# A gated recurrence in which every matrix product is cut into four 32-column groups of 128 columns, r and z take seven block products for eight, and a list scheduler orders the engines

## The chip, the core and the metric

The kernel runs on one core of one Trainium2 chip. A core has five engines with an instruction queue each: TensorE (PE, matrix products), VectorE (DVE), ScalarE (ACT), GpSimd (POOL) and SyncE (SP, which here only issues transfers). Queues run side by side and are worked off in order; semaphores join them. The metric is device time in microseconds, and lower is better. All data are 32-bit floats.

A matmul takes a stationary operand (here up to 128 rows by 32 columns, loaded by a LDWEIGHTS) and streams a moving operand of N columns past it. The kernel always uses 32 stationary columns, because half of the batch has 32 rows. Four such products can stand side by side in TensorE, each in its own *column group* of 32 columns, and each writes its own quarter of the 128 partitions of PSUM. A 32-bit matmul stands in the trace as two records, each with a weight load.

## The reference

Batch 64, 128 time steps, input and hidden width 512. With `comb = [x_t, h]`:

```python
def step(h, inp):
    x_t, prop = inp
    comb = jnp.concatenate([x_t, h], axis=-1)
    z = jax.nn.sigmoid(comb @ Wz + bz)
    r = jax.nn.sigmoid(comb @ Wr + br)
    comb2 = jnp.concatenate([x_t, r * h], axis=-1)
    h_cand = jnp.tanh(comb2 @ Wh + bh)
    h_new = (1.0 - z) * h + z * h_cand
    h_next = jnp.where(prop, jnp.tanh(h_new @ Wp + bp), h_new)
    return (h_next, h_new)
```

`prop` holds in every fourth step but the last. The result is `x` plus all `h_new`. The part with `x_t` of the three gates doesn't depend on `h` and can be worked out ahead; the part with `h` is a chain of 128 steps.

## The kernel before, in words

**Layout.** The batch is two halves of 32 rows (`S = 2`, `V = 32`), the hidden width four quarters of 128 columns (`NQ = 4`, `J = 128`). A state tile is 128 partitions (32 rows times four quarters) by two halves by 128 columns. K, the 512 rows of a weight, is four blocks of 128.

**The recurrence.** `half(h)` (L777) is a generator that runs the whole chain for one half of the batch: gate r, then r times h and its 32x32 transposition (L794, L244), gate z, gate of the candidate, the new state (L831, L840) and its transposition, and in every fourth step the propagation with `wp`. `gate` (L224) calls `products` (L213) for each of four blocks of K; `products` issues two matmuls of 256 columns (L215) into the two column groups 2h and 2h+1. One half of the batch therefore fills two of the four groups, and the other half has the other two. `seed` (L377) copies the prepared part of x into the PSUM bank ahead of the gate (L380). `crossed` (L239) applies sigmoid or tanh in two calls of 64 partitions, which bring the partitions back to the state's layout (L241).

**The part with x.** Steps 0 to 3 and the last ones use plain products (`plain`, L435: 48 matmuls a step). All other steps are done in groups of four (`Q4`) by a block scheme used twice, one inside the other, with seven products for eight: 49 block products for a group. `batch` (L453) runs two outer products at a time, each with seven inner ones, as matmuls of 192 columns into the banks `scratch`; ACT and DVE add the seven results up (L484, L501, L502, L507, L510, L511), and POOL makes the outer sums, with the biases, into `cp` (L542, L547). The sums of x that go into the products are POOL's too (`four`, L307).

**Order.** The two generators are interleaved by hand: at each yield the half with fewer columns issued so far goes on, with a lag of 700 columns (L868). Between the gates each half puts batch units into its own two groups (`fill`, L398), as many as the tables `PLACES`, `HEAD` and `TAIL` (L590) say for the step of the period of eight. Work of POOL and DVE is placed by step in `join` and `behind_step`. Loads of x are blocks of four steps, stores of the result likewise, all issued by SP except for some at the start that POOL and ACT issue.

Of the kernel before, what the change touches and what calls it, by code (L numbers as in the profile page):

```python
# [11 lines left out]
U16 = mybir.dt.uint16  # L12
AF = mybir.ActivationFunctionType
ALU = mybir.AluOpType
PSUM = bass.MemoryType.PSUM


@with_exitstack
def kernel(
# [14 lines left out]
    nc = tc.nc  # L34
# [8 lines left out]
    K = D // P  # L43
    Q4 = 4
    CHUNK = 4
    FIRST = 2
    LAST = T // Q4 - 1
# [3 lines left out]

    const = ctx.enter_context(tc.tile_pool(name="const", bufs=1))
    xrp = ctx.enter_context(tc.tile_pool(name="xr", bufs=2))  # L60
    one = ctx.enter_context(tc.tile_pool(name="one", bufs=1))
    xtp = ctx.enter_context(tc.tile_pool(name="xt", bufs=2))
    mbp = ctx.enter_context(tc.tile_pool(name="mb", bufs=3))
    two = ctx.enter_context(tc.tile_pool(name="two", bufs=2))
# [3 lines left out]
    zeros = one.tile([P, 4 * J], BF16, tag="cq", name="zeros")  # L68
    nc.vector.memset(zeros, 0.0)
    ones = const.tile([1, V], F32, name="ones")  # L70
    nc.gpsimd.memset(ones, 1.0)

    wx = const.tile([P, K, 3, H], F32, name="wx")
    wh = [const.tile([P, K, H], F32, name=f"wh_{i}") for i in range(3)]
    wp = const.tile([P, K, H], F32, name="wp")

    tw = {n: const.tile([P, S, NQ, 3, J // 2], F32, name=f"tw_{n}") for n in (2, 3, 4, 5)}
    tf = {n: const.tile([P, NQ, 3, J // 4], F32, name=f"tf_{n}") for n in (1, 2, 3)}
    tt = const.tile([P, 7, 3, NQ, 3, J // 4], F32, name="tt")
    gates_in = (Wr, Wz, Wh)  # L80

    bias_row = tt.rearrange("p a b c d e -> p (a b c d e)")[0:1, : 3 * H].rearrange(
        "p (i n) -> p i n", i=3
    )
# [4 lines left out]
    def load_x(tile_, t0, n):  # L89
        for h in range(S):  # L90
            for q in range(NQ):
                nc.sync.dma_start(
                    out=tile_[part(q), 0:n, h, :], in_=x[ts(h, V), t0 : t0 + n, ts(q, J)]
                )

    def load_step(t, engs):
        for q in range(NQ):
            engs[q % len(engs)].dma_start(
                out=xr[0][part(q), t], in_=x[:, t, ts(q, J)].rearrange("(h b) j -> b h j", h=S)
            )  # L100

    def load_wx(wt, w, k0=0, k1=K):
        nc.sync.dma_start(  # L103
            out=wt[:, k0:k1, :], in_=w.rearrange("(p k) n -> p k n", k=K)[:, k0:k1]
        )

    def load_wh(wt, w, engs=(nc.sync,)):
        for q in range(NQ):
            engs[q % len(engs)].dma_start(  # L109
                out=wt[part(q)], in_=w[ts(q, P), :].rearrange("(k e) n -> e k n", e=V)  # L110
            )

    xr = {}

    def new_xr(g):
        xr[g] = xrp.tile([P, Q4, S, J], F32, tag="xr", name=f"xr_{g}")

    h_init = two.tile([P, S, J], F32, tag="h", name="h_init")
    bias_x = const.tile([P, C, S, 3, J // 2], F32, name="bias_x")
    bias_p = const.tile([P, S, J], F32, name="bias_p")  # L120
    new_xr(0)
    load_step(0, (nc.sync, nc.scalar))
    for k in range(0, K, 2):
        load_wx(wx[:, :, R, :], gates_in[R][:D], k, k + 2)
    for i in (Z, H_):
        load_wx(wx[:, :, i, :], gates_in[i][:D])

    load_step(1, (nc.gpsimd,))
    for i, b in enumerate((br, bh, bz)):
        nc.gpsimd.dma_start(out=bias_row[:, i, :], in_=b.rearrange("(o n) -> o n", o=1))  # L130
    for t in (2, 3):
        load_step(t, (nc.gpsimd,))
    for h in range(S):
        nc.gpsimd.dma_start(
            out=h_init[:, h, :],
            in_=h0[ts(h, V), :].rearrange("b (q j) -> q b j", q=NQ),
        )

    nc.gpsimd.tensor_copy(wh[R][0:1, 0, 0:1], wx[0:1, K - 1, H_, 0:1])
    for i in range(3):  # L140
        load_wh(wh[i], gates_in[i][D:], (nc.sync, nc.gpsimd))

    dummy = const.tile([1, 1], F32, name="dummy")
    nc.scalar.activation(dummy, ones[:, 0:1], AF.Sigmoid)

    xs = {}

    def load_xs(g):
        if g * Q4 < T:
            xs[g] = one.tile([P, Q4, S, J], F32, tag=f"xs{g % 2}", name=f"xs_{g}")  # L150
            load_x(xs[g], g * Q4, Q4)

    new_xr(1)
    load_x(xr[1], Q4, Q4)
    load_xs(2)
    load_wh(wp, Wp)
    for q in range(NQ):
        nc.sync.dma_start(
            out=bias_p[part(q)],
            in_=bp.rearrange("(o d c j) -> c o d j", o=1, d=2, c=2)[q % 2].broadcast_to(  # L160
                [V, S, J]
            ),
        )


    P_ = 3
    rec = [ps_c.tile([P, 2, 2, J], F32, name=f"rec_{n}") for n in ("0", "1", "z")]
    z = rec[2][:, 1]

    def gate_ps(i, h):  # L170
        return rec[2][:, 0] if i == Z else rec[h][:, 0 if i == R else 1]

    scratch = [ps_c.tile([P, 4 * J], F32, name=f"scratch_{n}") for n in "qraxy"]
    q_ps, r_ps, a_ps, *x_two = (
        s[:, : 3 * J].rearrange("p (m h v) -> p m h v", m=2, h=S) for s in scratch
    )
    q_bank, r_bank, a_bank, *x_banks = range(5)
    r_ = scratch[r_bank][:, 3 * J :]

    def quarters(v):  # L180
        return v.rearrange("p n (d c j) -> p c n d j", d=2, c=2)

    def spread(bank, rows, which):
        bank = bank.rearrange("p (i d j) -> p i d j", i=2, d=2)
        for h in range(S):
            for c in range(2):
                nc.tensor.matmul(
                    bank[part(2 * h + c), 0 : len(which)],
                    lhsT=ones,
                    rhs=quarters(bias_row[:, rows])[:, c],  # L190
                    start=True,
                    stop=True,
                )
        for j, i in enumerate(which):
            nc.scalar.copy(
                bias_x[:, :, :, i, :].rearrange("p n d u -> p d n u"),
                bank[:, j].rearrange("p d (n u) -> p d n u", n=C),
            )

    bias0 = bias_x[:, 0]  # L200
    bias_d = const.tile([P, S, 3, J // 2], F32, name="bias_d")

    def idle(n):
        for i in range(n):
            nc.tensor.matmul(
                rec[i // NQ % 3].rearrange("p a d n -> p (a d n)")[part(i % NQ)],
                lhsT=zeros[:, :V],
                rhs=zeros,
                start=True,
                stop=True,  # L210
            )

    def products(ps, h, left, rhs, start=False):  # L213
        for c in range(2):
            nc.tensor.matmul(  # L215
                ps[part(2 * h + c)],
                lhsT=left,
                rhs=rhs(c),
                start=start,
                stop=True,  # L220
                skip_group_check=True,
            )

    def gate(i, h, lT, w):  # L224
        for k in range(K):
            products(gate_ps(i, h), h, lT[:, h, ts(k, V)], lambda c: quarters(w)[:, c, k])
            yield S * J

    def product(ps, h, lT, w, k, start=False):
        c0, s0 = divmod(k, C)  # L230
        products(
            ps.rearrange("p (d j) -> p d j", d=2),
            h,
            lT[:, c0, s0 * B + h * V : s0 * B + (h + 1) * V],
            lambda c: quarters(w)[:, c, k],
            start,
        )

    def crossed(dst, h, i, func):  # L239
        for d in range(2):  # L240
            nc.scalar.activation(dst[ts(d, 2 * V)], gate_ps(i, h)[ts(h, 2 * V), d, :], func)  # L241

    def turn(dst, src):
        nc.vector.transpose(out=dst, in_=src)  # L244

    def new_T(tag, name):
        return two.tile([P, S, P], F32, tag=tag, name=name)

    xT = {}

    def join_x(g, i):
        if g * Q4 >= T:
            return
        if g not in xT:
            xT[g] = xtp.tile([P, Q4, C, P], F32, tag="xT", name=f"xT_{g}")
        src = xr[g] if g < FIRST else xs[g]
        nc.vector.transpose(
            out=xT[g][:, i].rearrange("p c (a h b) -> p h (c a) b", a=S, h=S),
            in_=src[:, i].rearrange("p h (e k) -> p h k e", k=K),
        )  # L260

    def outer(kb, nb, ka):
        return wx[:, kb * S + ka, :, :].rearrange("p g (q n u) -> p n q g u", q=NQ, n=C)[:, nb]

    OPERAND = {
        1: lambda ka: outer(0, 0, ka),
        2: lambda ka: outer(1, 0, ka),
        3: lambda ka: outer(1, 1, ka),
        4: lambda ka: tw[4][:, ka],
        5: lambda ka: tw[5][:, ka],  # L270
# [649 lines left out]
```

## Time and profile before

| | |
|---|---|
| runs | 1275.79, 1276.58, 1276.74 us; median 1276.58 |
| span of the profiled execution | 1273.0 us, 60669 instructions |
| mean granted TensorE clock | 0.997 |
| busy share | PE 99%, weight loads 90%, DVE 63%, ACT 66%, POOL 71% |
| DMA | 60.82 MB, mean 48 GB/s |

The profile is one execution. The page gives only its span (first to last instruction) and no time of its own beside it; 1273.0 us stand against the runs above. In a group's row stand the source line, engine, operation, output and input tiles with their shapes and the count, then busy time and the mean duration of one in ns, then idle time of the engine before them and what ended it. A row of a stretch has its bounds, its length, the busy time and count of PE, of weight loads, DVE, ACT and POOL, then the granted clock, the DMA share and GB/s. A row of a timeline has start, duration, engine, line and operation, and in brackets the idle time before it. Rows of waits have the total, how many, and the longest. A matmul's record starts when it starts, but its end is modelled: in a stream of matmuls the distance of two starts is what one costs.

### The profile page before, as it was taken

How to read it: one execution, taken by the hardware profiler on the slowest of the kernel's cores; microseconds unless marked ns; L12 is line 12 of the kernel's file. 1: busy time of each engine (PE TensorE's matmuls, PEld its weight loads, DVE VectorE, ACT ScalarE, POOL GpSimd, SP SyncE). 2: the span in 40 equal slices, each digit the busy share in tenths (PEclk: the TensorE clock that was granted, in tenths of full speed). 3: DMA queues.
4: the chain of work that ended last, by engine and by line, in shares of the span. 5: the costliest groups of instructions: out<-in, count | busy, mean ns of one | idle time of the engine just before them, and what ended most of it. 6: DMA issues, size and time to landing. Idle time of an engine off the chain costs nothing.

```text
span 1273.0 us, 60669 instructions
## 1 busy us (share of the span) xinstructions
PE 1255.9 (99%) x25954; PEld 1150.3 (90%) x25954; DVE 800.4 (63%) x2153; ACT 835.5 (66%) x2685; POOL 906.0 (71%) x1053
## 2 busy tenths in 40 slices
PE   7899999999999999999999999999999999999998
PEld 4699999999999999999999999999999999999885
DVE  2765666666666666666666665666666666666544
ACT  1356666766666666676666667666666666666665
POOL 8788767777677786777687677776777777677530
PEclk9999999999999999999999999999999999999999
DMA  8302212102121111211111121111111112111010
GB/s 233 76 19 53 52 41 60 40 24 49 53 53 36 36 47 42 53 36 44 49 32 53 46 59 37 29 43 53 53 37 37 48 39 52 37 52 35 4 50 21
DMA packets 112212, 60.82 MB, mean 48 GB/s; under 512 B 12776, under 2 KB 108520, under 8 KB 111944
## 3 DMA queue, kind: packets, MB, share of 16 engines
q1 hardware_dynamic: 110532, 54.71, 16.5%
q8 instruction: 205, 3.36, 1.1%
q0 software_dynamic: 1120, 2.11, 0.7%
q14 instruction: 63, 0.52, 0.1%
q10 hardware_dynamic: 292, 0.13, 0.0%
HBM read 40.11 MB, written 16.78 MB: 45 GB/s over the span
## 4 chain that ended last, share of the span: by engine, by line
PE 95%; DMA 2%; DVE 1%; issue 1%; SPq 0%; ACT 0%; POOL 0%; POOLq 0%; DVEq 0%
PE rec L215 43%; PE rec_z L215 16%; PE scratch_r L215 14%; PE scratch_q L215 10%; PE scratch_a L215 5%; PE scratch_x L215 4%; PE scratch_y L215 4%; DMA wh<-in_L_cond_Wh_dram 1%; DMA wx<-in_L_cond_Wh_dram 1%; DVE tw L292 0%; DVE tw L293 0%; DVE tw L291 0%; SPq L109 0%; ACT rec_z L241 0%; SPq L103 0%
## 5 line engine op out<-in xcount | busy, mean ns | idle before, releaser
L215 PE MATMUL rec<-wh,rhT 128*32 128x256 f32 x4096 | 373.2, 379 | 0.0
L215 PE MATMUL rec<-wh,hT 128*32 128x256 f32 x3072 | 281.1, 381 | 4.9 <-DVE hT L244 4.7
L215 PE MATMUL rec_z<-wh,hT 128*32 128x256 f32 x3072 | 280.0, 379 | 0.1
L215 PEld LDWEIGHTS rec<-wh,rhT 128*32 128x32 f32 x4096 | 241.2, 110 | 23.4 <-ACT scratch_r L241 1.3
L241 ACT ACTIVATE scratch_r<-rec 64x128 f32<-64x128 f32 x512 | 128.0, 250 | 136.0 <-PE rec L215 68.1
L380 ACT COPY rec<-cp 64x256 f32<-64x256 f32 x512 | 189.8, 371 | 23.6 <-DVE cp L418 4.2
L215 PEld LDWEIGHTS rec<-wh,hT 128*32 128x32 f32 x3072 | 175.0, 110 | 27.3 <-ACT rec L380 6.4
L215 PEld LDWEIGHTS rec_z<-wh,hT 128*32 128x32 f32 x3072 | 184.8, 110 | 7.3 <-issue 0.6
L241 ACT ACTIVATE rec_z<-rec_z 64x128 f32<-64x128 f32 x512 | 128.0, 250 | 93.7 <-PE rec_z L215 81.6
L241 ACT ACTIVATE c<-rec 64x128 f32<-64x128 f32 x512 | 139.3, 272 | 60.1 <-PE rec L215 48.9
L215 PE MATMUL scratch_r<-tw,s 128*32 128x192 f32 x1392 | 166.0, 326 | 0.0
L752 POOL TENSOR_TENSOR xr<-xr,h 128x256 f32<-128x256 f32 x127 | 93.2, 734 | 89.6 <-DVE h L840 89.6
L542 POOL TENSOR_TENSOR mb<-mb,mb 128x768 f32<-128x768 f32 x58 | 106.3, 1833 | 66.4 <-DVE mb L511 66.4
L542 POOL TENSOR_TENSOR cp<-mb,mb 128x768 f32<-128x768 f32 x76 | 139.2, 1832 | 18.7 <-ACT scratch_r L241 9.4
L542 POOL TENSOR_TENSOR cp<-mb 128x768 f32<-128x768 f32 x46 | 84.3, 1834 | 59.7 <-ACT rec_z L380 58.3
L810 DVE SCALAR_TENSOR_TENSOR keep<-rec_z,h 128x256 f32<-128x256 f32 x96 | 40.8, 425 | 123.6 <-ACT rec_z L241 122.5
L484 ACT COPY cq<-scratch_q 128x384 f32<-128x384 f32 x212 | 102.3, 482 | 19.4 <-PE scratch_q L215 17.8
L501 DVE TENSOR_TENSOR cx<-scratch_r,cx 128x384 f32<-128x384 f32 x106 | 58.5, 552 | 74.3 <-PE scratch_r L215 40.3
L215 PE MATMUL scratch_q<-tt,s 128*32 128x192 f32 x928 | 101.9, 326 | 0.0
L215 PEld LDWEIGHTS scratch_r<-tw,s 128*32 128x32 f32 x1392 | 90.7, 110 | 7.7
L507 DVE TENSOR_TENSOR mb<-scratch_q,cx 128x384 f32<-128x384 f32 x106 | 58.8, 555 | 58.8 <-ACT cq L484 58.8
L794 DVE TENSOR_TENSOR rh<-scratch_r,h 128x128 f32<-128x128 f32 x192 | 56.0, 292 | 62.3 <-ACT scratch_r L241 62.3
(168 smaller groups left out, 3718.0 us busy)
## 6 DMA issues: line engine op xcount, KB each, us to landing
out_dram<-xr SPq DMA_DIRECT2D x249, 64.0 KB, 1.8
xr<-in_x_dram SPq DMA_DIRECT2D x248, 64.0 KB, 2.1
xs<-in_x_dram SPq DMA_DIRECT2D x240, 64.0 KB, 2.1
wx<-in_L_cond_Wr_dram SPq DMA_DIRECT2D x2, 512.0 KB, 5.5
wx<-in_L_cond_Wz_dram SPq DMA_DIRECT2D x1, 1024.0 KB
wx<-in_L_cond_Wh_dram SPq DMA_DIRECT2D x1, 1024.0 KB
wp<-in_L_cond_Wp_dram SPq DMA_DIRECT2D x4, 256.0 KB, 6.2
wh<-in_L_cond_Wr_dram SPq DMA_DIRECT2D x2, 256.0 KB, 4.3
```

What stands on the lines that cost most here:

```text
L215: nc.tensor.matmul(ps[part(2 * h + c)], lhsT=left, rhs=rhs(c), start=start, stop=True, skip_group_check=True,)
L241: nc.scalar.activation(dst[ts(d, 2 * V)], gate_ps(i, h)[ts(h, 2 * V), d, :], func)
L380: nc.scalar.copy(gate_ps(i, h)[rows].rearrange("p d (c n) -> p d c n", c=C), G[t][rows, :, :, i, :].rearrange("p c d n -> p d c n"),)
L484: nc.scalar.copy(c[:, :nm], ps[:, :nm])
L501: nc.vector.tensor_add(T2[what][:, :nm], r_ps[:, :nm], T2[what][:, :nm])
L507: nc.vector.tensor_add(blocks(1, 1), runs(q_ps[:, :nm]), runs(T2[what][:, :nm]))
L542: nc.gpsimd.tensor_add(dst, a, b)
L752: nc.gpsimd.tensor_add(xr[g][:, j], xr[g][:, j], h_new)
L794: nc.vector.tensor_mul(rh[:, h, :], r_, h_old[:, h, :])
L810: nc.vector.scalar_tensor_tensor(out=keep, in0=z, scalar=1.0, in1=h_old, op0=ALU.subtract, op1=ALU.mult)
```

## The change

Nearly the whole body is rewritten. What it does:

- *Four groups for each product.* A product of 32 rows with one block of K is four matmuls of 128 columns, one for each column group (`product_k`, `plain`), and a batch product is four matmuls of 96 columns for each half. Gate results thus stand in the state's layout: one activation call reads all 128 partitions.
- *Seven for eight.* From step 4 on, r and z of both halves are one block product: left, the two halves of the batch (`e`, `l`) by two halves of K; right, the weights of r and z by two halves of K. `gates_seven` uses seven block products with four differences of the state on POOL (`sa`), sums of weights made once (`s1`, `wt`, and `wh` of z overwritten by a difference), and six sums on DVE. Steps 0 to 3 keep `gates_plain`.
- *Batches.* Sums inside a batch are now partly made by seeding a PSUM bank with a copy of another (ACT) and accumulating on top; three of seven batches have their biases seeded into the banks, which takes most of POOL's bias sums away. Only steps 0 to 3 have plain products of x; the last group is a batch too.
- *Order.* Every operation is an `Op` of a `Plan` with engine, estimated cost, the data that it reads and writes, PSUM banks, and a due time in steps. `close` finds the dependences, `order` goes through the operations engine by engine: it takes the one that is due first among those that can start soonest, favours the chain (`main`) by 0.3 steps, keeps batch units back that are due more than one step after the next chain operation of PE, and lets an engine wait a little for a chain operation rather than begin a long one. Then all are emitted in that order, and each engine's order is fixed.
- *Transfers.* x is loaded for one step and half at a time, once for the products (`xj`) and once for the result (`xo`), each in a ring of four; results are stored by step and half.

```diff
-    def products(ps, h, left, rhs, start=False):
-        for c in range(2):
-            nc.tensor.matmul(
-                ps[part(2 * h + c)],
-                lhsT=left,
-                rhs=rhs(c),
...
-    def crossed(dst, h, i, func):
-        for d in range(2):
-            nc.scalar.activation(dst[ts(d, 2 * V)], gate_ps(i, h)[ts(h, 2 * V), d, :], func)
...
-    LAG = 700
-    halves = [half(0), half(1)]
...
+class Plan:
...
+    def order(self, patience, ahead, favour):
...
+        def urgency(op):
+            return op.due - (favour if op.main else 0.0) - op.rank
...
+                    if n < len(line_):
+                        limit = line_[n].due + ahead
+                        line = [op for op in line if op.main or op.due <= limit]
...
+                starts = [(begin(op), op) for op in line]
+                early = min(s for s, _ in starts)
+                picks = [(urgency(op), op.index, s, op) for s, op in starts if s <= early + 0.03]
...
+    COST = {
+        "dve": {64: 0.23, 128: 0.325, 256: 0.45, 384: 0.585},
+        "act": {128: 0.30, 256: 0.40, 384: 0.51},
+        "pool": {64: 0.36, 96: 0.40, 128: 0.48, 192: 0.60, 256: 0.76, 384: 1.1, 768: 1.86},
+    }
...
+    def product_k(ps, lT, w, ks, start, reads=(), writes=(), banks=""):
+        def emit():
+            for n, (kl, kw) in enumerate(ks):
+                for q in range(NQ):
+                    dst, right = ps[part(q)], w[:, kw, ts(q, J)] if w is not None else s1(kw)[:, q]
+                    if w is None:
+                        dst = dst.rearrange("p (d u) -> p d u", d=2)
+                    mm(dst, lT[:, ts(kl, V)], right, start and n == 0)
+
+        plan.due += 0.01
+        add("pe", 0.219 * len(ks), emit, reads, writes, banks, main=True)
...
+                    def unit(left=left, right=right, m=m, first=first):
+                        for h in range(S):
+                            for q in range(NQ):
+                                mm(ps[bank][part(q), m, h].rearrange("p (g u) -> p g u", g=3),
+                                   left[:, ts(h, V)], right[:, q], first and h == 0)
...
+        seeded("q", bias_q)
+        product("q", 1, bias is None)
+        copy(ps["a"], ps["q"], [key["q"]], [key["a"]], "q +a")
+        seeded("r", bias_r)
+        product("r", 5, bias is None)
+        copy(c5, ps["r"], [key["r"]], [("c5", n)], "r")
+        product("q", 6, False)
+        product("a", 2, False)
+        copy(block(0, 0), runs(ps["a"]), [key["a"]], blocks(0, 0), "a")
+        copy(ps["x"], ps["q"], [key["q"]], [key["x"]], "q +x")
+        copy(q2, ps["q"], [key["q"]], [("q2", n)], "q")
...
+    def gates_seven(t):
...
+        seed(cn(R_), xpart(t, R, 1), gx[R], [("R", 0)], "r")
+        product_k(B_, e, wh[R], first, True, reads=he + wk(R, 0, 1), writes=[("B", 0), ("E", 0)], banks="+b")
+        plus(cn(A_), cn(B_), xpart(t, R, 0), [("B", 0)] + gx[R], [("A", 0)], "b +e")
+        product_k(A_, e, wh[R], second, False, reads=he + [("A", 0)] + wk(R, 2, 3), writes=[("A", 0)], banks="+e")
+        reset(t, 0)
+        s(0, l[:, :B], e[:, :B], he + hl)
+        s(1, l[:, B:], sa[:, 0], hl + [("sa", t, 0)])
+        product_k(R_, l, S4, [(2, 0), (3, 1)], False, reads=hl + [("R", 0), ("T", 0, 4)], writes=[("R", 0)], banks="+r")
+        plan.due += 0.01
+        el("act", 128, lambda: nc.scalar.copy(c2_(t), R_), [("R", 0)], [("c2", t)], "r", main=True)
+        p(E_, "E", 0, None, [("T", 0, 1)])
+        p(B_, "B", 1, S2, [("T", 0, 2)])
+        plus(c2_(t), E_, c2_(t), [("E", 0), ("c2", t)], [("c2", t)], "b")
+        plus(R_, B_, c2_(t), [("B", 0), ("c2", t)], [("R", 0)], "b +r")
+        s(2, l[:, B:], l[:, :B], hl)
+        s(3, e[:, B:], sa[:, 1], he + [("sa", t, 1)])
+        reset(t, 1)
+        p(B_, "B", 2, wh[Z][:, 0:KH], [("T", 0, 3)])
+        plus(cn(c3_(t)), cn(E_), xpart(t, Z, 1), [("E", 0)] + gx[Z], [("c3", t)], "b")
+        plus(zz[:, 1], B_, c3_(t), [("B", 0), ("c3", t)], [("z", 0, 1)], "b +z")
+        p(B_, "B", 3, wh[Z][:, KH:K], wk(Z, 2, 3))
+        plus(cn(zz[:, 0]), cn(B_), xpart(t, Z, 0), [("B", 0)] + gx[Z], [("z", 0, 0)], "b +z")
...
+    plan.close()
+    plan.order({"pool": (0.1, 3.0), "dve": (0.15, 0.7), "act": (0.15, 0.5), "pe": (0.05, 0.08)}, 1.0, 0.3)
+    stats(plan)
+    for op in plan.done:
+        op.emit()
```

The products of `gates_seven` are called by their banks below: product 1 (`B_`, state `e`), the second r product (`A_`), the S4 product (`R_`, state `l`), E and B2 (`E_`, `B_` with `sa` 0 and 1), and the two last ones into `B_` for z. A *unit* is the eight matmuls of one batch product for both halves.

More of the change, by code (lines that the diff above doesn't have):

```diff
@@ L18, with stats @@
+def stats(plan):
+    import os, pickle
+    if os.environ.get("PLAN_OUT"):
+        pickle.dump([(o.engine, o.cost, o.start, o.end, o.main, o.index, sorted(o.after), o.name) for o in plan.done],
+                    open(os.environ["PLAN_OUT"], "wb"))
 @with_exitstack
@@ L113 @@
[L113 to L126, printed above, removed]
@@ L143 @@
[L143 to L161, printed above, removed]
-            ),
-        )
@@ L243, in turn, with mm @@
[L243 to L259, printed above, removed]
+    def mm(dst, lhsT, rhs, start):
+        nc.tensor.matmul(dst, lhsT=lhsT, rhs=rhs, start=start, stop=True, skip_group_check=True)
```

1434 lines of the change are left out of this document (817 added, 617 removed), and 4 rows, old and new, of the table RINGS.

## The prediction

> **What bounds the kernel now.** I read the engine totals first, then the chain that ended last, then the stretches of the span, and last the single matmuls.
>
> ```profile
> PE 1255.9 (99%) x25954; PEld 1150.3 (90%) x25954; DVE 800.4 (63%) x2153; ACT 835.5 (66%) x2685; POOL 906.0 (71%) x1053
> PE 95%; DMA 2%; DVE 1%; issue 1%; SPq 0%; ACT 0%; POOL 0%; POOLq 0%; DVEq 0%
> ```
>
> TensorE is busy for 99% of the span and is 95% of the chain. A busy PE need not be one at its peak, so the stretches (time, PE busy, weight loads, DVE, ACT, POOL, clock) come next.
>
> ```profile
> 0.00:6.50 6.50, 4.63 (x42) 1.60 (x42) 0.92 (x2) 1.49 (x2) 5.14 (x14) 1.00 0.63 176
> 6.50:46.00 39.50, 30.15 (x492) 17.85 (x496) 18.54 (x30) 7.36 (x24) 31.62 (x34) 0.96 0.86 213
> 130.00:1130.00 1000.00, 1000.00 (x20980) 935.24 (x20976) 647.37 (x1753) 683.13 (x2192) 734.87 (x858) 1.00 0.17 44
> 1220.00:1273.00 53.00, 47.23 (x842) 35.26 (x834) 24.73 (x78) 30.25 (x105) 10.30 (x10) 0.99 0.11 27
> ```
>
> From 130 to 1130 us PE never idles; a record takes 47.7 ns of the span. Lost time lies at the head and in the last steps. What does one record cost when all four groups of 32 columns work? Two places tell: plain products at the head (256 columns) and a stretch where both halves run batches (192 columns; ten such rows stand from 52.01 to 53.47, each with one record for each of two groups).
>
> ```profile
> 14.53 1.91 PE L215 MATMUL scratch_a<-wx,xT 128*32 128x256 f32 x32
> 16.25 1.26 PE L215 MATMUL scratch_r<-wx,xT 128*32 128x256 f32 x20
> 52.01 0.36 PE L215 MATMUL scratch_x<-tt,s12r 128*32 128x192 f32 x2
> 53.47 0.36 PE L215 MATMUL scratch_r<-tf,s12r 128*32 128x192 f32 x2
> ```
>
> 256 columns: 1.72 us for 32 records, 53.8 ns each, 215 ns in one group. 192 columns: 1.46 us for nine periods, 162 ns in one group, 40.6 ns for each record. So a record costs 0.207 ns a column plus 0.8 ns, shared by four groups. By the loops the kernel has 13,856 records of 256 columns (two for each of 6,928 matmuls) and 12,040 of 192: 745 + 488 = 1,234 us of matmul in a span of 1,273. The bound is the number of columns streamed, and 39 us are lost around it.
>
> **The change, part by part: matmul time.** Seven products of two weight blocks replace r's and z's eight from step 4 on: 56 matmuls of 128 columns where 64 would stand. With candidate (32 a step), propagation (31 times 32), four plain steps (384) and four steps of x (384) that is 12,672 matmuls, 25,344 records. The batches are 1,526 units of eight matmuls of 96 columns, 24,416 records. No record of 128 or 96 columns is in this trace. By the line above they cost 27.3 and 20.7 ns: 692 + 505 = 1,197 us, **37 us less**. (The eighth product is worth 124 x 16 x 27.3 ns = 54 us; twice as many records give back some 19 us of the constant.) In the steady part that is 74.4 us for eight steps, against 76.6 us of records now.
>
> From below, the same columns cannot be cheaper than 0.207 ns each, which would save the 40 us of constants more. From above stand 215/4 = 54 ns a record, if a record had no price below 256 columns, which is 2,690 us; nearer floors are a rival below. I take the line, because the next rows show neither issue nor weight load as slow as 20 ns.
>
> ```profile
> 45.44 0.31 DVE L244 STREAM_TRANSPOSE hT<-h 128x128 f32<-128x128 f32 x1
> 45.67 0.27 DVE L831 TENSOR_TENSOR rec_z<-c,rec_z 128x128 f32<-128x128 f32 x1
> 45.90 0.41 PE L215 MATMUL rec<-wh,hT 128*32 128x256 f32 x2 [4.75 <-DVE hT L244]
> 45.91 0.41 PE L215 MATMUL scratch_a<-wx,xT 128*32 128x256 f32 x2
> 45.93 0.11 PEld L215 LDWEIGHTS rec<-wh,hT 128*32 128x32 f32 x1
> 45.94 0.12 PEld L215 LDWEIGHTS scratch_a<-wx,xT 128*32 128x32 f32 x2
> 45.98 0.29 DVE L840 TENSOR_TENSOR h<-rec_z,keep 128x128 f32<-128x128 f32 x1
> 600.95 0.39 PE L215 MATMUL rec_z<-wh,hT 128*32 128x256 f32 x2
> 601.39 0.25 ACT L241 ACTIVATE rec_z<-rec_z 64x128 f32<-64x128 f32 x1 [0.31 <-PE rec_z L215]
> ```
>
> After a wait, four matmuls start within 0.02 us, and second weights begin 0.03 us later, each group for itself. The same rows price a handoff. The transposition ends at 45.75, the matmul starts at 45.90: **0.15 us into PE**. Last matmul's start to its reader is **0.44 us** at 256 columns; at 128 the record is 106 ns shorter, so 0.33. A 128-column product over two blocks of K is 4 x 109 = 0.44 us of PE and 0.66 us from its start to its reader; over four blocks 0.87 and 1.09. DVE instructions follow each other after some 0.03 us.
>
> **The other engines.** Rows for the durations:
>
> ```profile
> L244 DVE STREAM_TRANSPOSE hT<-h 128x128 f32<-128x128 f32 x254 | 79.2, 312 | 8.8
> L507 DVE TENSOR_TENSOR mb<-scratch_q,cx 128x384 f32<-128x384 f32 x106 | 58.8, 555 | 58.8 <-ACT cq L484 58.8
> L794 DVE TENSOR_TENSOR rh<-scratch_r,h 128x128 f32<-128x128 f32 x192 | 56.0, 292 | 62.3 <-ACT scratch_r L241 62.3
> L810 DVE SCALAR_TENSOR_TENSOR keep<-rec_z,h 128x256 f32<-128x256 f32 x96 | 40.8, 425 | 123.6 <-ACT rec_z L241 122.5 <-PE rec L215 1.0
> L241 ACT ACTIVATE scratch_r<-rec 64x128 f32<-64x128 f32 x512 | 128.0, 250 | 136.0 <-PE rec L215 68.1 <-DVE mb L510 52.8 <-DVE cx L501 1.5
> L380 ACT COPY rec_z<-cp 128x256 f32<-128x256 f32 x128 | 48.2, 377 | 55.7 <-DVE h L840 52.5 <-DVE cp L418 2.2 <-POOL cp L542 1.0
> L484 ACT COPY cq<-scratch_q 128x384 f32<-128x384 f32 x212 | 102.3, 482 | 19.4 <-PE scratch_q L215 17.8
> L542 POOL TENSOR_TENSOR cp<-mb,mb 128x768 f32<-128x768 f32 x76 | 139.2, 1832 | 18.7 <-ACT scratch_r L241 9.4 <-DVE mb L511 5.8
> L547 POOL TENSOR_TENSOR mb<-mb,bias_x 128x768 f32<-128x768 f32 x34 | 62.3, 1831 | 28.3 <-DVE mb L511 28.3
> L311 POOL TENSOR_TENSOR s4r<-xT 128x64 f32<-128x64 f32 x29 | 9.5, 327 | 0.0
> ```
>
> DVE gains six 128-column sums a step (nearest row 292 ns): 124 x 6 x 0.292 = 217 us, and loses three of five 384-column sums for each of 106 batches (318 x 0.555 = 176 us): 841 us busy, and with some 2,570 gaps of 0.03 us 918, or 7.2 us a step. ACT gains three copies a batch and 90 copies that seed biases into banks (408 x 0.48 = 197 us), and loses half of its activations, because a call now reads all 128 partitions at once (seven fewer a step, 128 x 7 x 0.25 = 224 us): about even. POOL loses some 60 bias sums (110 us) and gains four 64-column subtractions a step for the seven products (496 x 0.327 = 162 us). SP issues 788 transfers for 765, loads in rings of four tiles well ahead of use. None of these passes PE's 9.35 us a step (1,197/128), so I cost them at nothing as work; PE hides them. If that cover goes, they cost through the recurrence, which is next.
>
> **The recurrence.** The kernel orders each engine beforehand, so I follow one step. In the instruction order a middle step is: product 1, a batch unit (0.33 us), the S4 product, the second r product, E, B2, a unit, candidate of the first half, a product, a unit, candidate of the second half, the last product, then some eight units. From the last product (start) to the next step's first: reader 0.66, z sum 0.29, sigmoid 0.36 (between 250 and 377 ns), keep 0.43, product 0.29, difference 0.29, transposition 0.31, gaps 0.2, into PE 0.15, together 3.0 us. PE has the product itself (0.44) and eight units (2.65): 3.1, covered. The S4 product waits for the second half's new state, which DVE delivers three instructions (0.98 us) later; product and one unit cover 0.77, so 0.2 is open where one unit stands there, nothing where two do. E's operand takes POOL 0.33 us from the same state, and E starts 0.87 us after S4: covered, as long as POOL isn't in a 1.83 us sum. Candidate one: second r product 0.66, sigmoid 0.28, product 0.32, transposition 0.31, into PE 0.15, sum 1.7 after its start; PE has 3 x 0.44 + 0.33 = 1.65. So 0.2 to 0.3 us are open; I take 0.25 for each of 116 steps, **29 us**. Ends: none (the middle stretch now), and 1.2 us a step, if all eight handoffs paid 0.15.
>
> The last batch is due by step 123, so the last four steps stand bare. Their loop: into PE 0.15, product 0.66, sum 0.29, into PE 0.15; B2 starts 0.87 later, 2.1. Reader 2.8, DVE first ends r's first half, then two sums, 3.4; sigmoid, product, transposition, into PE: 4.5. Candidate 0.87, last product's reader 0.66: 6.0; then sum, sigmoid, keep, product, difference, transposition with gaps: 8.2 us. PE's work in it is 88 x 2 x 27.3 ns = 4.8 us, so 3.4 us x 4 = **14 us** idle.
>
> Head: the first matmul waits for the same transfers (6.5 us). Then come all four plain x steps, 21 us of work, during which the recurrent weights land; now PE waits for these instead.
>
> ```profile
> PE rec L215 <- DMA wh<-in_L_cond_Wr_dram: 2.8, 1, 2.8
> PE scratch_q L215 <- DMA wx<-in_L_cond_Wr_dram: 1.4, 2, 0.8
> ```
>
> I keep 4 us for loads and 6 us for steps 0 to 3, which stand almost without batch units; ends 2 and 20 (now: 39.5 us with 492 x 53.8 ns = 26.5 us of work). After the last matmul 6 us, as now.
>
> **The sum.** 6.5 + 1,197 + 4 + 6 + 29 + 14 + 6 = 1,263 us of span, against 1,273.0. The page gives the profiled execution no time beside its span; the span stands 3.6 us below the median of the runs (1,276.58), so I predict **1,267 us**. A measurement of this kernel can tell about 0.2%, 2.6 us, from no change.
>
> **Rivals.**
>
> Slower: *DVE brings the turned state late.* One queue, loaded for 7.2 of 9.35 us a step, now carries six more sums a step in a fixed order; one 0.55 us evacuation in front of a transposition, of which PE covers 0.1, lifts the open time from 0.25 to 0.70 us a step: +52 us, 1,319. It decides from 0.35 us a step on, where the 10 us gained are gone. For it: DVE's waits in the rows above are for ACT, so it works just in time. Against: DVE has idle time in every step.
>
> *All handoffs are covered*: no open time in the middle, 1,263 - 29 = 1,234, 1,238 us. For it: the middle stretch now idles nowhere. Against: four dependent products stand without a unit between them.
>
> *A floor under short records.* No stretch sustains closer starts than 40.6 ns. If nothing were gained below 128 columns, or if a group could not load weights faster than a load's record lasts (0.11 us, 27.5 ns over four groups), a 96-column record would cost 27.3 ns or more: 24,416 x 6.6 = 161 us, 1,428. Against both: four starts within 0.02 us at 45.90, and second loads 0.03 us behind the first matmuls. [...]
>
> **How the numbers follow.** Forecast 0.46 (its own range 1,250 to 1,284: open time 0.1 to 0.4 us), DVE late 0.28 (1,279 to 1,335), all covered 0.13 (1,228 to 1,250), floor 0.13. Range 1,232 to 1,335: it leaves out the floor and some 0.05 of the covered case. Faster: 0.37 of the forecast and the 0.13 covered, 0.50; same: 0.06 of the forecast and 0.02 of the late case, 0.08; slower: 0.03, 0.26 and 0.13, 0.42.
>
> **What will show it.** 256-column records are gone, 128-column starts in a group lie 109 ns apart and 96-column ones 83 ns; at 100 ns or more a floor is there. PE's busy time in the middle falls to about 97%, waits before it name DVE transpositions. The last four steps take 8.2 us each. The prediction fails if short records do not follow the line, or if open time is over 0.35 us a step.

## The result and the profile after

The changed kernel takes 1,556.9 us (1,553.8 to 1,558.6) beside 1,276.6 us for the kernel before on the same chip: a ratio of 1.2195, 95% interval 1.2178 to 1.2212. It is 22% slower. The prediction said 1,267 us and a range that ended at 1,335.

The page of the changed kernel: engine totals, two rows of the DMA queues (packets, MB, share), and the chain that ended last.

```profile
span 1553.5 us, 108778 instructions
PE 1336.3 (86%) x49826; PEld 1221.7 (79%) x49826; DVE 846.0 (54%) x2591; ACT 662.7 (43%) x2021; POOL 947.2 (61%) x1497
q8 instruction: 391, 6.41, 1.8%
PE 79%; issue 10%; SPq 3%; ACT 3%; DVE 2%; DMA 1%; POOL 1%; POOLq 0%; DVEq 0%; ACTq 0%
```

TensorE was 95% of the chain and is 79%. Two things are new. "issue", time in which the engine waited for nothing that the profile shows, went from 1% to 10%; SP's queue, which was 0%, has 3%. The row of queue q8, which the page names "instruction", is one that the prediction never looked at: 391 packets of 16 KB. I read them as the blocks in which TensorE's own instructions come: the trace has 100,107 instructions on TensorE's queue, 256.0 for each packet. The kernel before has 205 packets and 52,482 instructions, 256.0 again:

```profile
q8 instruction: 205, 3.36, 1.1%
```

Stretches of the changed kernel (bounds, length, busy time and count of PE, weight loads, DVE, ACT and POOL, clock, DMA share, GB/s), then PE's waits:

```profile
10.00:30.00 20.00, 18.11 (x561) 16.36 (x557) 12.82 (x19) 1.42 (x5) 14.35 (x16) 1.00 0.55 165
37.00:67.00 30.00, 0.00 (x0) 0.00 (x0) 0.00 (x0) 0.59 (x3) 0.00 (x0) 0.57 0.28 97
130.00:1130.00 1000.00, 892.21 (x33778) 818.53 (x33769) 569.15 (x1767) 458.21 (x1392) 634.99 (x1015) 1.00 0.14 39
```

```profile
PE ps_e L360 <- ACT ps_e L847: 33.3, 2, 30.5
PE ps_x L360 <- issue: 29.0, 45, 1.2
PE ps_q L360 <- issue: 25.6, 41, 1.4
PE ps_y L360 <- issue: 21.2, 37, 1.1
```

There are two separate losses. In the steady part a thousand microseconds now hold 33,778 records, 29.6 ns each, where the prediction's line gives 24 for the mixture of 128 and 96 columns; the idle time in between stands under "issue". And at 37 to 67 us PE does nothing at all, behind one instruction of ACT.

What one of the "issue" pauses looks like, in a stretch of PE's timeline (start, duration, what, count, idle time before):

```profile
801.72 0.54 PE L360 MATMUL ps_q<-tw,xT 128*32 128x96 f32 x16 [0.31 <-issue]
...
802.74 0.84 PE L360 MATMUL ps_x<-tt,o 128*32 128x96 f32 x32
803.39 0.51 PE L360 MATMUL ps_y<-tw,s 128*32 128x96 f32 x16
...
805.47 0.54 PE L360 MATMUL ps_q<-tt,s 128*32 128x96 f32 x16 [0.79 <-issue]
...
807.02 0.62 PE L360 MATMUL ps_b<-wx,sa 128*32 128x128 f32 x16
807.46 0.62 PE L360 MATMUL ps_b<-wt,sa 128*32 128x128 f32 x16
...
808.26 0.65 PE L360 MATMUL ps_e<-wh,rhT 128*32 128x128 f32 x16
809.49 0.65 PE L360 MATMUL ps_e<-wh,rhT 128*32 128x128 f32 x16 [0.58 <-issue]
```

The pauses end at 801.72, 805.47 and 809.49, and the third falls in the middle of one product (`ps_e<-wh,rhT`, 16 records before it and 16 behind it), whose turned operand was there for the first half already. Between one end and the next stand exactly 128 records each time: with their weight loads 256 instructions, one block (49,826 records and as many weight loads, over 391 blocks, are 255). Between the pauses the records keep to the prediction's line: 16 records of 128 columns in 0.44 us, 27.5 ns each, and 32 of 96 columns in 0.65 us, 20.3 ns each. So between the pauses TensorE computes as fast as forecast; that it then stands until its next instructions have come is my reading, which e1 to e3 test. The pattern is not one of this stretch alone: counted along TensorE's queue (matmuls, weight loads and semaphore instructions), all 246 "issue" pauses of over 0.15 us between 130 and 1,480 us end at the same place of a count of 256 (to one instruction), and 214 of the 259 us that the prediction's line leaves over there stand at that place. From 130 to 1,480 us the blocks' transfers start 3.75 us apart (median; 3.4 to 4.3 hold nine tenths), which is **29 ns a record, at 96 columns as at 128**. In the kernel before they start 6.0 us apart (median), and PE has no "issue" pause in the steady part.

Where the time stands, by a sum like the prediction's. Records are told apart by their output bank and each is priced by the prediction's line; the rest of a stretch is the difference. e1 is an experiment below. The first row ends where the prediction had the first matmul of x; in the changed kernel that one starts at 10.8 us, behind matmuls that spread the biases, and the 4.3 us between count in the third row.

| us | predicted | after | e1 |
|---|---|---|---|
| first 6.5 us | 6.5 | 6.5 | 6.5 |
| all records by the line | 1,197 | 1,197 | 1,188 |
| rest, 6.5 to 130 us | 10 | 57 | 52 |
| rest, 130 us to 50 us before the last matmul | 29 | 263 | 61 |
| rest, last 50 us | 14 | 23 | 22 |
| after the last matmul | 6 | 7 | 7 |
| span | 1,263 | 1,553.5 | 1,336.1 |

### The profile page after: what moved, and what is told of

It is laid out like the page before. It is cut to its first block, busy times and chain, and to the rows that moved or that the text cites. A ratio compares the mean times of both kernels' runs of the same rounds, so it can differ in the third digit from the quotient of the medians.

```text
span 1553.5 us, 108778 instructions
## 1 busy us (share of the span) xinstructions
PE 1336.3 (86%) x49826; PEld 1221.7 (79%) x49826; DVE 846.0 (54%) x2591; ACT 662.7 (43%) x2021; POOL 947.2 (61%) x1497
## 4 chain that ended last, share of the span: by engine, by line
PE 79%; issue 10%; SPq 3%; ACT 3%; DVE 2%; DMA 1%; POOL 1%; POOLq 0%; DVEq 0%; ACTq 0%
PE ps_b L360 18%; PE ps_r L360 14%; PE ps_e L360 14%; PE ps_q L360 10%; PE ps_x L360 9%; PE ps_y L360 9%; PE ps_a L360 5%; SPq L403 2%; SPq L385 1%; DMA wp<-in_L_cond_Wp_dram 1%; ACT ps_z L851 1%; ACT ps_a L699 1%; POOL cp L732 0%; ACT cand L851 0%; ACT ps_e L847 0%
## 5 line engine op out<-in xcount | busy, mean ns | idle before, releaser
L360 PE MATMUL ps_b<-wh,sa 128*32 128x128 f32 x3968 | 175.4, 274 | 6.5 <-issue 4.6
L360 PE MATMUL ps_e<-wh,rhT 128*32 128x128 f32 x4096 | 152.5, 276 | 9.3 <-issue 5.0
L360 PE MATMUL ps_r<-wh,rhT 128*32 128x128 f32 x4096 | 151.0, 275 | 9.3 <-issue 5.3
L360 PEld LDWEIGHTS ps_b<-wh,sa 128*32 128x32 f32 x3968 | 123.9, 109 | 14.9 <-issue 13.0
L360 PE MATMUL ps_e<-wh,hT 128*32 128x128 f32 x2112 | 99.2, 279 | 40.3 <-ACT ps_e L847 30.5
L360 PEld LDWEIGHTS ps_r<-wh,rhT 128*32 128x32 f32 x4096 | 116.7, 110 | 21.0 <-issue 10.7
L805 DVE STREAM_TRANSPOSE hT<-h 128x128 f32<-128x128 f32 x318 | 99.1, 312 | 61.8 <-ACT h L851 51.4
L360 PEld LDWEIGHTS ps_e<-wh,rhT 128*32 128x32 f32 x4096 | 116.2, 110 | 18.9 <-issue 11.0
L360 PE MATMUL ps_y<-tw,s 128*32 128x96 f32 x2912 | 110.0, 247 | 9.1 <-issue 9.0
L360 PE MATMUL ps_b<-wx,sa 128*32 128x128 f32 x1984 | 94.4, 277 | 5.6 <-issue 4.8
## 6 DMA issues: line engine op xcount, KB each, us to landing
wx<-in_L_cond_Wr_dram SPq DMA_DIRECT2D x4, 256.0 KB
wh<-in_L_cond_Wr_dram SPq DMA_DIRECT2D x4, 256.0 KB
wh<-in_L_cond_Wz_dram SPq DMA_DIRECT2D x4, 256.0 KB
```

The source lines that it names most:

```text
L360: nc.tensor.matmul(dst, lhsT=lhsT, rhs=rhs, start=start, stop=True, skip_group_check=True)
L805: add("dve", 0.345, lambda: nc.vector.transpose(out=dst, in_=src), reads, writes, main=True)
```

## The experiments

Theory *supply*: TensorE gets 256 instructions in some 3.75 us at best (the median above), and the narrow matmuls need them faster. Rivals: *handoffs* (the order leaves gaps, the prediction's "DVE late"), and a *fixed price* for each record. Beside them the *head*: the 30 us behind ACT's instruction.

**e1: half as many instructions for the batches, the same columns.**

```diff
-                            for q in range(NQ):
-                                mm(ps[bank][part(q), m, h].rearrange("p (g u) -> p g u", g=3),
-                                   left[:, ts(h, V)], right[:, q], first and h == 0)
+                            for c in range(2):
+                                mm(ps[bank][part(2 * h + c), m].rearrange("p h (g u) -> p h g u", g=3),
+                                   left[:, ts(h, V)], right[:, c::2], first)
```

> The changed kernel, but each batch unit is four matmuls of 192 columns in two column groups for each half in place of eight of 96 in four: the same column time (12,208 records x 40.6 = 496 us against 505), the same order, waits and sums, half of the batch instructions. The batch results land in other places, so the values are not the reference's. Theory of the instruction supply (256 TensorE instructions, one block of 16 KB, cannot follow each other in less than some 3.75 us): 294 blocks x 3.75 = 1,100 us is under the 1,190 us of matmul, so the time falls from 1,557 to about 1,300 us (1,280 to 1,330; what the head of the changed kernel loses stays). Rival, handoffs in a fixed order: nothing about them changes, 1,530 to 1,560 us.

Measured: 1,338.4 us, ratio to before 1.0495 (1.0477 to 1.0512). Every operation of the other engines, every dependence and the scheduler's order are those of the changed kernel, and 218 us are gone; the record's constant explains 12,208 x 0.8 ns = 10 of them. Its page:

```profile
PE 1255.9 (94%) x37618; PEld 1076.8 (81%) x37618; DVE 842.3 (63%) x2591; ACT 660.1 (49%) x2021; POOL 948.6 (71%) x1497
q8 instruction: 295, 4.83, 1.5%
PE 82%; ACT 4%; DVE 4%; SPq 4%; POOL 2%; issue 2%; DMA 2%; POOLq 0%; DVEq 0%; ACTq 0%
```

"issue" is back at 2%. That handoffs are the main loss is refuted. The time lies 38 us above the expected 1,300 and 8 above the end of its range: the head, which this edit leaves alone, and the open time in the middle (52 and 61 us in the table) are more than I had allowed.

**e2 and e3: the kernel before, cut narrower.** If supply is the cause, the old kernel must become slow when its matmuls are cut in two, with nothing else changed, and must not if only so many are cut that a block still lasts long enough.

```diff
-        for c in range(2):
-            nc.tensor.matmul(
-                ps[part(2 * h + c)],
-                lhsT=left,
-                rhs=rhs(c),
...
+        for d in range(2):
+            for c in range(2):
+                nc.tensor.matmul(
+                    ps[part(2 * h + c), d],
+                    lhsT=left,
+                    rhs=rhs(c)[:, d],
+                    start=start and d == 0,
...
```

e2 cuts all of them, e3 those of the gates alone.

> The kernel before, with each matmul cut in two of half its columns in the same column group: same order, same waits, same results, twice the TensorE instructions (104,000, 405 blocks). Instruction supply: 405 x 3.75 = 1,520 us and some 10 at the head, about 1,530 us. The prediction's line (0.8 ns for each further record): 1,277 + 20 = 1,297 us. A fixed price of some 10 ns for each further record (what the changed kernel lost, spread over its records): 1,537 us.

> The kernel before, with the matmuls of the recurrent gates alone cut in two (6,640 more matmuls, 13,280 more records, 307 blocks). Instruction supply: 307 x 3.75 = 1,150 us lies under the 1,236 us of matmul, so only the 0.8 ns count: 1,285 us (1,277 to 1,300). A fixed price of 10 ns for each further record: 1,277 + 133 = 1,410 us.

Measured: e2 1,580.2 us (two runs, 1,569.5 and 1,590.9), ratio 1.2382 (1.2285 to 1.2479); e3 1,293.8 us, 1.0132 (1.0117 to 1.0147). Pages of e2 and then of e3:

```profile
q8 instruction: 407, 6.67, 1.8%
PE 87%; issue 10%; DMA 2%; ACT 0%; DVE 0%; SPq 0%; POOL 0%; POOLq 0%; DVEq 0%
```

```profile
PE 1275.1 (99%) x39234; PEld 1225.9 (95%) x39234; DVE 803.6 (62%) x2153; ACT 834.8 (65%) x2685; POOL 905.2 (70%) x1053
q8 instruction: 308, 5.05, 1.7%
```

e2 is slower than the changed kernel, without its scheduler, its seven products or its head; its blocks start 3.76 us apart (median). It is 40 to 60 us above the 1,530 expected from the supply, so that sum was too low, and alone it would not tell the supply from a fixed price (1,537 expected). e3 has 13,280 records more than the kernel before and costs 17 us, 1.3 ns for each, near the line's constant of 0.8; its blocks start 4.00 us apart (median). A fixed price of 10 ns for a record would have shown in e3 as well as in e2. The loss sets in between the two: from 130 to 1,130 us a record takes 29.6 ns in e2 (33,816 records, PE busy for 906 us), with the pauses, and 32.0 ns in e3 (31,284 records, busy for 999 us), nearly without.

**e4: streams without any wait.** The same pair of operands, four groups in turn, in sections of one width each.

```diff
+    for kind, width, count in (("f", 256, 768), ("f", 192, 768), ("f", 128, 768), ("f", 96, 768),
+                               ("f", 64, 768), ("f", 32, 768), ("b", 512, 1536), ("b", 128, 1536)):
...
+            nc.tensor.matmul(ps[q * 32 : q * 32 + 32, 0:width], lhsT=l[:, q], rhs=r[:, 0:width],
+                             start=True, stop=True, skip_group_check=True)
```

> Nothing but streams of matmuls with no waits, in the four column groups in turn, 768 32-bit matmuls (1,536 records) each of 256, 192, 128, 96, 64 and 32 columns, then 1,536 16-bit ones of 512 and of 128 columns; x is copied to the output and the rest of the computation is left out. Instruction supply: 54, 40.6 ns a record, then 29 ns for all four smaller widths, with a pause after each 128 records, and 16-bit 128 columns 29 ns too. The prediction's line: 53.8, 40.6, 27.3, 20.7, 14.0 and 7.4 ns.

Measured (454 us in one run): over its whole section a record takes 55.0 ns at 256 columns, 40.6 at 192, 27.8 at 128, 28.3 at 96, 28.1 at 64 and 29.1 at 32; in bf16 55.0 at 512 columns and 27.3 at 128. PE's timeline:

```profile
203.20 2.85 PE L55 MATMUL f<-right,left 128*32 128x96 f32 x128 [0.88 <-issue]
206.66 2.84 PE L55 MATMUL f<-right,left 128*32 128x96 f32 x128 [0.61 <-issue]
...
243.39 1.99 PE L55 MATMUL f<-right,left 128*32 128x64 f32 x128 [1.46 <-issue]
246.84 1.99 PE L55 MATMUL f<-right,left 128*32 128x64 f32 x128 [1.46 <-issue]
...
287.36 1.93 PE L55 MATMUL f<-right,left 128*32 128x32 f32 x128 [2.07 <-issue]
...
416.71 1.97 PE L55 MATMUL b<-rb,lb 128*32 128x128 bf16 x128 [1.50 <-issue]
```

From 96 to 32 columns the time hardly moves: 128 records, then a pause. From 96 to 64 columns the pause grows by what the records save; at 32 the records themselves are hardly faster (1.93 us after 1.99), and the granted clock averaged 0.54 in that section (0.943 over the run). 128 records take 3.46 and 3.45 us at 96 and 64 columns in these rows (203.20 to 206.66, 243.39 to 246.84), and 3.45 to 4.02 us in all rows of 96 columns and fewer, with nothing else running; in the changed kernel the median was 3.75. Narrowing a matmul below 128 columns thus bought nothing in these streams. In the section of 128 columns, the first 1,370 records ran without a pause, and in bf16 the first 220, which is why both stay under the 29 ns expected. No run shows why; a section as short as that would have shown no limit.

**e5, e6: the head.** ACT's queue has the seed of step 3's propagation, which reads `bias_p`, ahead of the work of step 0. SP issues `bias_p` last of the weights, at 54 us, behind transfers that each hold its queue for 0.8 to 3 us:

```profile
25.50 11.98 SPq L403 DMA_DIRECT2D wh<-in_L_cond_Wh_dram  x4
37.52 13.41 SPq L385 DMA_DIRECT2D xo<-in_x_dram  x8
50.98 3.27 SPq L403 DMA_DIRECT2D wp<-in_L_cond_Wp_dram  x4
54.29 4.32 SPq L1057 DMA_DIRECT2D bias_p<-in_L_cond_bp_dram  x4
```

e5 moves `bias_p` and `wp` ahead of `xo`; e6 also loads the recurrent weights by quarters of the partitions.

```diff
+    for q in range(NQ):
+        load("sp", lambda q=q: nc.sync.dma_start(
+            out=bias_p[part(q)],
...
+    for k in range(K):
+        load_wh(wp, Wp, ("wp", 0), k)
...
-    load_rest()
```

```diff
-                out=dst[:, k, :], in_=w.rearrange("(q k e) n -> k q e n", q=NQ, k=K)[k]
...
+                out=dst[part(q)], in_=w[ts(q, P), :].rearrange("(k e) n -> e k n", e=V)
```

> Edit: the kernel after, with the loads of the propagation's bias and of wp issued ahead of the loads of x for the result, so that the seed that stands early in ScalarE's queue (bias_p into ps_e, 30.5 us of TensorE waiting at 37 to 67 us) finds its data. Head theory: the stall shrinks to what the slow weight loads leave; 15 to 30 us go, 1,527 to 1,542 us against 1,557. Rival (the stall is only the nearest name for loads that all come late, so the next one takes its place): 0 to 10 us go, 1,547 to 1,557.

> Edit: e5, and each recurrent weight loaded in four transfers by quarters of the 128 partitions (as the kernel before does) in place of four by blocks of K with the quarters inside one transfer. Head theory: transfers then move at some 200 GB/s in place of 105, TensorE's idle stretch at 37 to 67 us goes nearly whole: 30 to 36 us less than the kernel after, 1,521 to 1,527 (1,510 to 1,535). Rival (the rate is set by the mix of x rows and weights, not by the form of the weight loads): the same time as e5.

Measured: e5 1,552.8 us, ratio 1.2162 (1.2139 to 1.2185); e6 1,530.9 us, 1.2003 (1.1983 to 1.2023). Waits in e5, of PE over the span and of DVE before 90 us:

```profile
PE ps_e L360 <- DVE rhT L813: 37.3, 2, 36.4
DVE xT L468 <- DMA xj<-in_x_dram: 52.0, 7, 37.7
```

The name that the wait bore misled me. With the bias early, ACT's seed runs at 20 us, and PE stands as long as before: now for DVE, whose queue has a transposition of x of the next group (`xj`, issued from 62 us on) ahead of step 0's state and waits 37.7 us there. e5's rival holds; it gained 4 us. What cures the stretch is the form of the loads. Stretches of e6:

```profile
10.00:30.00 20.00, 15.99 (x420) 14.31 (x421) 11.17 (x18) 2.58 (x10) 14.43 (x17) 0.91 1.00 239
37.00:67.00 30.00, 24.25 (x788) 22.64 (x781) 14.99 (x39) 6.37 (x23) 16.55 (x20) 0.93 0.23 59
```

239 GB/s and a DMA share of 1.00 at 10 to 30 us, beside 165 and 0.55 (and 97 at 37 to 67 us); PE is busy for 24 of the 30 us. 26 us are gone in all, a little less than the 30 to 36 expected; a new pause of 4.12 us in the head is told under the unexpected.

**e7: both repairs.** e6 with the wide units of e1.

> Edit: e6 with the batch units of e1 (192 columns in two groups for each half; values land elsewhere, so the time alone counts). If supply of instructions and the head are two separate causes, their gains add: 1,338 - 33 = 1,305 (1,292 to 1,318). Rival (they overlap, since a stream that is short of instructions catches up while TensorE waits): 1,320 to 1,338.

Measured: 1,318.1 us, ratio 1.0331 (1.0316 to 1.0347), at the end of the expected range and just under the rival's: the head's part is 20 us beside 26 in e6. So the two causes are nearly independent, and without both the change would still be 3% slower than the kernel before.

**e8: eight products for seven.** e7 with `gates_plain` in all steps.

```diff
-    SEVEN = 4
+    SEVEN = T
```

> Edit: e7 with r and z by eight products in all steps (the plain gates of steps 0 to 3 throughout): 16 records more in each of 124 steps, 1,984 in all, but six sums, four differences and three dependent products fewer. Columns alone: 1,984 x 27.3 ns = 54 us more than e7; at the supply rate of 29 ns, 58 us more. If the products' dependences are what costs, their going gives back up to 29 us (0.25 us for each of 116 steps): 25 to 58 us slower than e7 by the first theory. Rival (seven products cost in handoffs what they save in columns): e7 or less.

Measured: 1,445.1 us, ratio 1.1331 (1.1309 to 1.1353), 127 us more than e7, twice what the columns cost and outside what either side expected. This does not price the eighth product: the scheduler arranges the whole kernel anew, crowds the batch units between steps (from 608.3 us on PE has nothing else for 19 us), and PE waits in places where it did not:

```profile
PE ps_y L360 <- POOL s L543: 30.7, 14, 2.2
```

**e9 to e12: what is left of e7.** Its rest is 33 us before 130 us, 60 in the middle, 23 in the last 50. e9 and e10 correct the scheduler's prices for transfers and for a handoff, e11 has both; e12 takes two of ACT's copies of a batch away.

```diff
-    RATE = 350.0
+    RATE = 200.0
...
-        cost = {"sp": 0.1, "actq": 0.1, "pool": 0.55}[engine]
+        cost = {"sp": 0.75, "actq": 0.75, "pool": 0.55}[engine]
```

```diff
-    HOP = 0.06
+    HOP = 0.15
```

```diff
-        copy(ps["a"], ps["q"], [key["q"]], [key["a"]], "q +a")
...
-        product("a", 2, False)
+        product("a", 2, True)
...
-        copy(ps["x"], ps["q"], [key["q"]], [key["x"]], "q +x")
...
```

> Edit: e7 with the scheduler's prices for transfers raised towards what the trace shows: an issue 0.75 us in place of 0.1, 200 GB/s in place of 350. Between 6.5 and 130 us e7 spends 33 us that are not matmul time. If the wrong prices put waiting operations too early into the in-order queues, 8 to 20 us go: 1,298 to 1,310 against 1,318. Rival (the loads themselves set the head): within 5 us of e7.

> Edit: e7 with the scheduler's price of a handoff between engines at 0.15 us (what the trace of before shows into TensorE) in place of 0.06. Between 130 and 1,255 us e7 spends 60 us that are not matmul time. If they are handoffs that the order leaves open because it prices them too low, 15 to 40 us go: 1,278 to 1,303. Rival (they lie in the chain itself or in the supply, whatever the order): 1,308 to 1,328.

> Edit: the prices of e9 and of e10 together. If both theories hold the gains add: 1,258 to 1,295. If neither holds: within 10 us of e7's 1,318.

> Edit: e7 without the two copies of a batch by which ScalarE seeds one PSUM bank with another (q into a, q into x); the sums then lack these terms, so the time alone counts. In e7 TensorE stands 12 us before the units that follow these copies and 60 us in all between 130 and 1,255 us. If the copies' wait is a real part of the open time, 8 to 20 us go: 1,298 to 1,310 against 1,318. Rival (the scheduler moves the open time to other handoffs): 1,313 to 1,323.

Measured: e9 1,315.4 us (1.0313, 1.0297 to 1.0328), e10 1,337.6 (1.0481, 1.0464 to 1.0499), e11 1,334.1 (1.0455, 1.0439 to 1.0471), e12 1,316.0 (1.0313, 1.0296 to 1.0330). My theory falls in all four. e9 and e12 end where their rivals said; e10 and e11 are 16 to 20 us slower than e7, which neither side expected. In the middle of e7, then of e12 (130 to 1,255 us), PE's longest waits are

```profile
PE ps_q L360 <- ACT ps_a L708: 6.5, 28, 0.6
PE ps_y L360 <- ACT ps_y L708: 2.8, 13, 0.2
```

```profile
PE ps_e L360 <- ACT ps_r L854: 1.5, 9, 0.2
PE ps_r L360 <- ACT ps_r L854: 0.9, 5, 0.2
```

The copies' wait is gone in e12, yet the open time is 59 us after 60: it reappears in small pieces ahead of the products of the recurrence (15 us before product 1 of a step, 15 before the two candidates and 7 before the propagation; in e7 9, 13 and 3). e10's higher price for handoffs made an order in which PE waits for the turned state:

```profile
PE ps_e L360 <- DVE hT L814: 22.2, 13, 1.8
```

So some 0.5 us a step stays open in two orders (e7, e12), and a third is worse. What it would take to close it stays open; no experiment here shows it. No version beat the kernel before.

## Why the prediction was wrong, point by point

- **Matmul time, the line: right; the bound drawn from it: wrong.** In bursts 128 and 96 columns cost 27.5 and 20.3 ns a record against 27.3 and 20.7. The step that failed is "the next rows show neither issue nor weight load as slow as 20 ns". The four starts within 0.02 us at 45.90 came after a wait of 4.75 us, and four records say nothing of a long stream: in e4 128 of 64 columns run at 15.5 ns each, and with the pause behind them they take 28.1. The sum had no term for the supply of instructions: 25,954 records became 49,826. That term is 200 to 215 us: 218 that e1 gained less 10 for the constant, 263 less 61 in the table, or the 214 that stand where blocks change.
- **The floor rival** came nearest with 1,428 us, for a reason that is not the one found: neither the array nor the weight loads have that floor (64 columns run at 1.99 us for 128 records between pauses, 15.5 ns). But its observation, that no stretch sustained starts closer than 40.6 ns, was the clue, and the queue of instructions stood on the page.
- **Head: 10 us predicted, 57 measured.** What the prediction said of SP, "loads in rings of four tiles well ahead of use", costed at nothing, failed in the first 70 us. Also 4 of the 57 us are the first matmul of x, which starts at 10.8 us and not at the 6.5 of the forecast. I counted SP's transfers and did not ask how long SP takes for one, nor in what form the weights are loaded.
- **Open time: 0.25 us a step predicted, about 0.5 measured** once supply is out of the way (61 us in e1, 60 in e7). This is no rest of the supply: in e7 only some 6 of the 60 us stand where blocks change. 0.35 was the point from which the change loses, so by this estimate it would have lost with a supply without limits too. The rival "DVE late" (0.70 us a step, +52 us) is right in part only: where the semaphores of e7's trace name what came last, waits under 0.15 us counted, DVE's transpositions end some 14 of the 60 us and ACT's copies 26; in e12 DVE ends 22. e10 looks most like it. In the changed kernel itself 45 of the 259 us stand away from the block changes; what the order alone would cost there can't be told, since a pause also gives the other engines time.
- **Tail: 8.2 us a step predicted; 9.85 and 10.1 measured** (first products at 1,518.83, 1,528.68 and 1,538.79). The idle time ahead of a step is near the forecast (2.3 us after the last product, where its loop leaves some 2.5), but after it the granted clock is 0.50, which my sum did not have. The four products from 1,519.79 us on take 3.1 us, where the line has 1.75:

```profile
1516.60:1518.80 2.20, 0.00 (x0) 0.00 (x0) 1.64 (x6) 0.59 (x2) 0.00 (x0) 1.00 0.00 0
1519.80:1522.40 2.60, 2.60 (x52) 2.60 (x56) 0.47 (x2) 0.53 (x2) 1.86 (x5) 0.50 0.00 0
```

- **Other engines: right as to the bound.** DVE 846 us (841 predicted), POOL 947 (958 by the prediction's terms), ACT 663, lower than "about even" with 835; none of them is the bound.
- **The eighth product, 54 us: not tested cleanly** (e8). Of the 127 us that e8 adds, its 1,984 further records are 54 by the line; whether seven products pay in this chain is not shown.

## What to carry to other kernels

Count TensorE's instructions as well as its columns: in these runs a long stream of matmuls with a weight load each got 128 of these pairs in 3.45 to 4.02 us (e4) and in a median of 3.75 (the changed kernel), so records that the line prices at 20.7 and 27.3 ns turned columns saved into pauses under "issue" (29.6 ns a record in the changed kernel and in e2), while at 32.0 ns a record (e3) PE was busy for 999 of 1,000 us. Before believing a price for something shorter than the trace has, look for a stretch that sustains it, and read the instruction queue's row of the DMA table: span over blocks, 6.2 us before and 4.0 after (3.75 in the steady part), was the warning here. When an engine stands behind a late transfer, ask first what repairs the transfer: here moving the one that bore the blame brought the next one forward and gained 4 us (e5), and loading the weights in another form gained 26 (e6).

## What the runs showed that I had not expected

- *An instruction block came late while weights were loaded.* While the DMA share is 1.00 during e6's weight loads (10 to 30 us), no block's transfer starts between 20.1 and 30.1 us, and PE pauses for 4.12 us under "issue" before 33.00; in e7 one such pause lasts 4.96 us. Whether the weight loads hold the block back is not shown; no run separates it. From e6's timeline:

```profile
33.00 4.43 PE L360 MATMUL ps_a<-wx,xT 128*32 128x128 f32 x98 [4.12 <-issue]
```

- *The form of a weight load.* The same 256 KB with the quarters of the partitions inside one transfer moved at about 107 GB/s (DMA share 0.28, 30 to 37 us of the changed kernel), by quarters at 207 to 239 (0.99 to 1.00, 10 to 37 us of e6).
- *The granted clock stood at 0.50 after three short idle times.* Each of the last three steps of the changed kernel has 2.3 us without matmuls (2.28, 2.27 and 2.34), and from 0.4 to 0.9 us after their end the granted clock is 0.50 for 3.4 us (from 1,519.2, 1,529.4 and 1,539.7 us). The length alone does not decide: 2.49 us of idle time ahead of 1,510.45 us left the clock at 1.00 up to 1,518.80 us.
